# The order of loads around the first batch's attention products, and seven products in place of four tiles for the last group

## The chip, the cores and the metric

The kernel runs on one core of one Trainium2 chip. The metric is the device time of one execution in microseconds (us). The kernel before was timed in three runs: 520.41, 521.44 and 521.71 us, median 521.44 us. A separate execution was profiled.

## The reference

Four batches of 1024 tokens with 512 channels pass through one block, all in float32:

```python
mod = (silu(c) @ wmod).reshape(4, 6, 1, 512)          # sa, ca, ga, sb, cb, gb
h = layernorm(x) * (1 + ca) + sa
qf, kf = h @ Wq.T, h @ Wk.T                            # rank 64, the same for all heads
attn = softmax(qf @ kf.T)
x = x + ga * ((attn @ (h @ Wv.T)) @ Wo.T)
h = layernorm(x) * (1 + cb) + sb
x = x + gb * (sum_r(h @ factors[r]) / sqrt(8) + bias)   # eight factors of 512 x 512
```

`ga` and `gb` are first kept away from zero (at least 0.25 in size). All heads have the same scores, so attention is one matrix of 1024 x 1024 for each batch.

## The kernel before, in words

The kernel folds Wv and Wo into one matrix (`wvo`), and the eight factors into one sum (`fsum`). For a batch it makes LN1 (layer norm and modulation), the q and k projections, eight tiles of scores (128 tokens x 1024), softmax, P = the turned probabilities, Y = h(wvo*ga), O = P Y, then LN2 and F = h(fsum*gb). A tile is 128 tokens; tiles 0 to 3 of a batch are group 0, tiles 4 to 7 group 1.

**Products by sevens.** O and F are made in blocks of two by two with seven block products in place of eight (Strassen's scheme). For O a pair p = 0..3 of tiles has products (p,1), (p,5), (p,4), (p,6), (p,2), (p,3), (p,7); for F each group g has two pairs m = 0, 1. The seven share three PSUM banks: 1, 6, 7 and 4 accumulate one after another in bank "y" (which has two buffers, so the next pair's can begin), 5 and 3 in "q", and 2 in "x". After each product VectorE adds the bank's state to a quarter of x (L581 for O, L632 for F), so the next product of the same bank has to wait for that add. Products 5, 6 and 3 take sums of left blocks (`sum_probs` L502, `sum_h` L601: n = 0 for product 5, n = 1 for 6, n = 3 for 3; n = 2 overwrites the block that product 7 reads). Only the last batch's group 1 is made in another way: `f_tile` (L639) multiplies each of its four tiles plainly, four matmuls of 128x512 each, with one add of 128x512 (L648) and one store.

**Moves.** Transposing P or a normalised h takes a 32x32 transpose on VectorE (L491 for P, L378 for h) and then sixteen DMAs of 64 KB that move the 32x32 blocks (`move_blocks`, L374). They are issued by SyncE (SP), one queue, in program order. A batch has four moves of P (64 DMAs) and four of h (64 DMAs; the last two, of the last batch, are split between SP and ScalarE's queue). P and h moves of LN2 are made of 128 B packets.

**Buffers that tie things together.** The tag "pr" has three buffers: the probabilities of the four pairs and the staging tiles `st` of LN1 and LN2 rotate through them. So `st` of the next batch's group 0 takes the buffer of pair 1's probabilities, and group 1's that of pair 2, and ScalarE's first write there (L318, a sum over x) waits until that move of P has landed. Factors 2 and 3 live in two of the four "hT" buffers; LN2 of batch 0 takes these two buffers next.

**Order.** Every operation is put on a list with a beat (`at`, `pe`, `behind`), and `plan.run` sorts by beat; that order is the program order, hence the order of every engine's own queue. Engines run their queues in order. `behind` puts a tiny VectorE memset ("tick", L277) and a GpSimd copy of it ("mark", L279) ahead of GpSimd work, so that GpSimd doesn't start it before VectorE got there.

The loads that matter here, all in batch 0: SP issues x of batch 1 (eight DMAs of 256 KB, L114) at the end of `plan_start`, ahead of the P moves (L695). GpSimd (POOL) issues the factors (1 MB each, L261) and adds them to `fsum` (L264): factors 1 to 4 in `plan_start`, 5 to 7 in `plan_o` (L792 to L797). Factor 5 is loaded into factor 2's buffer, 6 into 3's, 7 into 2's again. `scale_w` (L286) makes the next batch's wvo*ga on POOL from `bc_ga`, a row that SP spreads over the partitions behind the P moves (L243). The reciprocal standard deviation of a layer norm (a power, L327 for LN1 and L339 for LN2) is taken on POOL, in its queue; for LN2 VectorE first adds epsilon (`rstd`, L337) and afterwards makes -mean*rstd (`center`, L344).

Of the kernel before, what the change touches and what calls it, by code (L numbers as in the profile page):

```python
# [37 lines left out]
def kernel(  # L38
# [52 lines left out]
    def psum_mm(name, tag=None):  # L91
        turn[0] += 1
        return psum(tag or "yqyx"[turn[0] % 4], 512, name)
# [160 lines left out]
    def load_factor(r):  # L254
        if r == 0:
            fac[r] = fsum
        elif r < 4:
            fac[r] = wide(*((wfp, "wf") if r == 1 else (hp, "hT")), f"factor_{r}")
        else:
            fac[r] = fac[{4: 1, 5: 2, 6: 3, 7: 2}[r]]  # L260
        nc.gpsimd.dma_start(out=fac[r], in_=factors[r].rearrange("(kc p) e -> p kc e", p=P))  # L261

    def add_factor(r, k):
# [67 lines left out]

    def stage(ln, b, g):
        st[ln, b, g] = prp.tile([P, NQ, KC, GT, Q], F32, tag="pr", name=f"st{ln}_{b}_{g}")

    def rstd(ln, b, g):
        v = small.tile([P, GT], F32, tag="rs_v", name=f"v{ln}_{b}_{g}")
# [299 lines left out]
            [a[:, k, ts(m, P)] for k in range(KH)], [f[:, k, :] for k in range(KH)], add,  # L636
        )

    def f_tile(b, t):  # L639

        g, j = divmod(t, GT)
        ps = psum_mm(f"ps_f_{b}_{t}")
        for kc in range(KC):
            nc.tensor.matmul(  # L644
                ps, hT[2, b, g][:, ds((kc * GT + j) * P, P)], fb[b][:, kc, :],
                start=(kc == 0), stop=(kc == KC - 1),
            )
        nc.vector.tensor_tensor(xt[b, t], ps, xt[b, t], ALU.add)  # L648

    def f_pair(g, m):  # L650
        return g * GT + m, g * GT + GT // 2 + m

    def store(b, t, queue):
        queue.dma_start(out=out[b, ts(t, P), :], in_=xt[b, t])  # L654

    def add_bias(b, t):
        nc.gpsimd.tensor_tensor(xt[b, t], xt[b, t], bcs["gbias", b], ALU.add)  # L657
# [3 lines left out]
    def plan_softmax(b, p, k):  # L661

        at(plan.now + 0.5, exponents, b, p, k)
        if k:
            at(plan.now + 7, turn_probs, b, p)
            at(plan.now + 8, move_probs, b, p)

    def plan_start():
        for g in range(2):
            s = 8.0 if g == 0 else 44.0  # L670
            for j in range(GT):
                at(s + 2 * j, stats, 1, 0, g * GT + j)
            at(s + 9, rstd, 1, 0, g)
            for j in range(GT):
                at(s + 10 + j, normalize_first, g * GT + j)
        pe(8, warm_up)
        for cc in range(KC - 1):
            pe(8, wvo_chunk, cc)
        pe(8, mod_products, [0, 1], "q")
        at(plan.now, mod_row, 1, nc.vector)  # L680
        at(plan.now, mod_row, 0, nc.scalar)
        pe(4, wvo_chunk, KC - 1, range(2))
        at(plan.now, wvo_out, 0)
        at(plan.now, wvo_out, 1)
        for m, plus in ((1, 1.0), (0, 0.0)):
            pe(1, channel_products, m)
            at(plan.now, channel, m, plus)
        pe(4, wvo_chunk, KC - 1, range(2, KC))
        for kc in range(KC):
            pe(1, turn_first, 0, kc)  # L690
            at(plan.now, first_out, 0, kc)
        at(plan.now, wvo_out, 2)
        at(plan.now, wvo_out, 3)
        for t in range(NT):
            at(plan.now + (22 if t < GT else 40), load_x, 1, t)  # L695
        for r in range(2):
            at(plan.now + 1, load_factor, r)
        at(plan.now + 21, after_gates)
        for r in range(1, 5):
            if r in (2, 3):  # L700
                at(plan.now + 21, load_factor, r)
            for h in range(2):
                at(plan.now + 14 * r + 8 + 6 * h, add_factor, r, ts(h, KC // 2))
            if r == 1:
                at(plan.now + 14 * r + 15, load_factor, 4)
        pe(8, project, 0, 0)
        at(plan.now, qk_out, 0, 0)
        for kc in range(KC):
            pe(1, turn_first, 1, kc)
            at(plan.now, first_out, 1, kc)  # L710
        pe(8, mod_products, [2, 3, 4, 5], "y")
        for m in (2, 5):
            at(plan.now, mod_row, m, nc.scalar)
            at(plan.now, gate_sign, m)
            if m == 2:
                at(plan.now, gate, m)
        for m in (3, 4):
            at(plan.now, mod_row, m, nc.scalar)
        at(plan.now + 0.1, gate_b)
        at(plan.now, publish, row(2), "ga")  # L720
        pe(8, project, 0, 1)
        at(plan.now, qk_out, 0, 1)
        pe(2, spread_first)
        for kc in range(KC):
            at(plan.now, scale_w, 0, kc, nc.vector)
# [39 lines left out]
    def plan_ln2(b, g, ready):  # L765

        for j in (GT - 2, GT - 1):
            at(ready, stats, 2, b, g * GT + j)
        at(ready + 0.5, rstd, 2, b, g)
        at(ready + 4, center, 2, b, g)  # L770
        for j in range(GT):
            eng = nc.scalar if b + 1 == B and (g or j % 2) else nc.vector
            at(ready + 5 + 2 * j, normalize, 2, b, g, j, eng)
        for c in range(NQ):
            at(ready + 13 + (2.6 if b + 1 == B else 2) * c, turn_h, 2, b, g, c)
        at(ready + (21.5 if b + 1 == B else 19.5), move_h, 2, b, g)
        for j in range(GT):
            behind(ready + (22 if b + 1 < B else 26) + 5 * j, add_bias, b, g * GT + j)
        for kc in range(KC):
            late = 46 + 4 * (kc // 2) * g if b + 1 < B else 31  # L780
            at(ready + late, shift_h, 2, b, g, kc, nc.scalar)

    def plan_o(b):
        s = plan.now
        if b + 1 < B:
            plan_ln1(b + 1, 0, s + 2, s + 20)
            plan_ln1(b + 1, 1, s + 21, s + 39)
            at(s, spread, "ga", b + 1)
            for kc in range(KC):
                behind(s + (92 if b == 0 else 60) + 6 * kc, scale_w, b + 1, kc, nc.gpsimd)  # L790
        if b == 0:
            at(s - 28, load_factor, 5)  # L792
            at(s + 14, load_factor, 6)
            at(s + 34, load_factor, 7)
            for r, beat in ((5, s + 3), (7, s + 48), (6, s + 74)):
                for kc in range(KC):
                    behind(beat + 6 * kc, add_factor, r, ts(kc, 1))  # L797
        at(s + 24, spread, "gbias", b)
        for n in range(4):
            at(s - (26 if b else 16) + 3 * n, sum_probs, b, 0, n)  # L800
            at(s + 2 + 4 * n if b else s + 2 * n, sum_probs, b, 1, n)
        for p in range(NP):
            if 0 < p < NP - 1:
                for n in range(4):
                    at(plan.now + 3 + 4 * n, sum_probs, b, p + 1, n)
            for n in (1, 5, 4, 6, 2, 3, 7) if p < NP - 1 else (1, 5, 4, 6, 2, 7, 3):
                if n != 4:
                    pe(4, o_product, b, p, n)
                elif p:
                    pe(4, o_product, b, p - 1, 4)  # L810
                    if p % 2:
                        for j in range(2):
                            at(plan.now + 2 + 4 * j, stats, 2, b, 2 * (p - 1) + j)
                    else:
                        plan_ln2(b, p // 2 - 1, plan.now + 2)
        pe(4, o_product, b, NP - 1, 4)
        plan_ln2(b, 1, plan.now + 1)

    def plan_f(b, groups):
        pairs = [(g, m) for g in groups for m in range(GT // 2)]  # L820
        queue = nc.gpsimd if b + 1 < B else nc.sync

        def done(t):
            at(plan.now + 2, store, b, t, queue)
            if b + 2 < B:
                at(plan.now + 12, load_x, b + 2, t, nc.gpsimd)

        def fourth(g, m):
            pe(2, f_product, b, g, m, 4)
            done(f_pair(g, m)[1])  # L830

        for i, (g, m) in enumerate(pairs):
            end = i + 1 == len(pairs)
            for n in (1, 5, 4, 6, 2, 3, 7) if not end else (1, 5, 4, 6, 2, 7, 3):
                if n != 4:
                    pe(2, f_product, b, g, m, n)
                    if n == 3:
                        done(f_pair(g, m)[0])
                elif i:
                    fourth(*pairs[i - 1])  # L840
        fourth(*pairs[-1])

    def plan_scale_f(b, spread_beat, beat, queue):
        at(spread_beat, spread, "gb", b, queue)
# [13 lines left out]
    for b in range(B):  # L858
# [15 lines left out]
        else:  # L874
            plan_scale_f(b, s - 170, s - 104, nc.gpsimd)
            plan_sums_f(b, s - 70, 6)
            plan_sums_h(b - 1, 1, s - 40, 5)
            plan_sums_h(b, 0, plan.now + 4, 3, nc.gpsimd)
            plan_f(b - 1, range(1, 2))
            plan_f(b, range(1))  # L880
            for t in range(GT, NT):
                pe(8, f_tile, b, t)
                at(plan.now + 2, store, b, t, nc.sync)
    with tc.manual_schedule():
        plan.run()

# [32 lines left out]
```

## Time and profile before

| what | us |
|---|---|
| runs of the kernel before, median of three | 521.44 |
| the profiled execution's own time | 521.12 |
| its span in the trace | 519.3 |
| PE (TensorE matmuls) busy | 503.8 |
| DVE (VectorE) busy | 366.9 |
| POOL (GpSimd) busy | 178.9 |
| ACT (ScalarE) busy | 172.1 |
| share of PE in the chain that ended last | 77% |
| share of SP's issues in that chain | 9% |

The trace starts when the first instruction starts. The page names engines PE, PEld (weight loads), DVE, ACT, POOL and SP; "SPq" is SP's queue issuing a DMA. "A<-B" in brackets after a row says how long the engine was idle before it and what ended the wait. PE is busy nearly throughout, so what matters is where it isn't, and at what clock it runs.

### The profile page before, as it was taken

What the parts mean: (1) busy time and instruction counts of PE and PEld (TensorE: products, weight loads), DVE (VectorE), ACT (ScalarE), POOL (GpSimd) and SP (SyncE); (2) the same over time, 40 slices, a digit from 0 to 9 for tenths busy, and PEclk for the clock granted to TensorE, in tenths of its full rate; (3) what the DMA queues carried; (4) which work ended last, traced back from release to release, by engine and by line L of the source; (5) the groups of instructions that cost most, each with busy time, mean ns of one, the idle gap of its engine ahead of it and who ended that gap; (6) DMA issues with size and microseconds to landing.
All of it is one profiled execution on the core that took longest, in us unless ns stands there. A gap on an engine that the chain in (4) does not pass through costs nothing.

```text
span 519.3 us, 6306 instructions
## 1 busy us (share of the span) xinstructions
PE 503.8 (97%) x1906; PEld 336.3 (65%) x1906; DVE 366.9 (71%) x728; ACT 172.1 (33%) x309; POOL 178.9 (34%) x240
## 2 busy tenths in 40 slices
PE   8999999779999999999999999999999999999997
PEld 4343437668733388888733388888733488888772
DVE  5358486289779966489679966589678975786631
ACT  1144434442265403452356304442256300012220
POOL 1027803335946013215535023215536015015620
PEclk9999999979999999999999999999999999999999
DMA  8977966964536679523536679533536776014542
GB/s 319 380 293 260 221 139 96 218 131 107 88 61 98 96 131 241 166 72 91 100 58 98 96 146 235 143 76 92 97 56 108 101 134 130 0 19 63 109 137 81
DMA packets 223154, 68.64 MB, mean 132 GB/s; under 512 B 206400, under 2 KB 206912, under 8 KB 223120
## 3 DMA queue, kind: packets, MB, share of 16 engines
q1 hardware_dynamic: 208112, 46.99, 46.1%
q0 software_dynamic: 5456, 19.14, 11.2%
q10 hardware_dynamic: 9552, 2.11, 2.1%
q8 instruction: 15, 0.25, 0.2%
q14 instruction: 19, 0.16, 0.1%
HBM read 28.33 MB, written 8.41 MB: 71 GB/s over the span
## 4 chain that ended last, share of the span: by engine, by line
PE 77%; SPq 9%; DVE 4%; ACT 3%; DMA 3%; issue 2%; POOL 0%; DVEq 0%; ACTq 0%; POOLq 0%
PE ps_o_y L564 20%; PE ps_y L521 14%; PE ps_o_q L564 9%; SPq L374 9%; PE ps_f_y L564 8%; PE ps_o_x L564 5%; PE ps_f_q L564 4%; PE ps_sc L468 4%; PE ps_qk L441 3%; PE ps_wvo L170 3%; PE ps_f L644 3%; PE ps_f_x L564 2%; PE ps_mod L189 1%; DMA hT<-st 1%; ACT st L356 1%
## 5 line engine op out<-in xcount | busy, mean ns | idle before, releaser
L521 PE MATMUL ps_y<-w,hT 128*128 128x512 f32 x256 | 117.0, 602 | 0.0
L521 PEld LDWEIGHTS ps_y<-w,hT 128*128 128x128 f32 x256 | 46.6, 190 | 66.7 <-issue 65.7
L394 ACT ACTIVATE hT<-hT,chan,chan 128x512 f32<-128x512 f32 x56 | 41.3, 803 | 99.3 <-DMA hT<-st 73.2
L564 PE MATMUL ps_o_y<-y,pt 128*128 128x256 f32 x256 | 61.2, 391 | 6.2 <-DVE x L581 6.2
L564 PEld LDWEIGHTS ps_o_y<-y,pt 128*128 128x128 f32 x256 | 50.4, 197 | 14.4 <-DVE x L581 6.6
L279 POOL COPY mark<-tick 1x1 f32<-1x1 f32 x72 | 17.2, 239 | 114.5 <-DVE tick L277 112.8
L482 ACT ACTIVATE pr<-ps_sc,nm 128x1024 f32<-128x1024 f32 x32 | 35.6, 1113 | 50.8 <-DMA pt<-pr 17.2
L581 DVE SCALAR_TENSOR_TENSOR x<-ps_o_y,ri,x 128x256 f32<-128x256 f32 x64 | 30.7, 480 | 30.8 <-PE ps_o_y L564 29.0
L654 POOL DMA_DIRECT2D out_dram<-x x24 | 13.3, 556 | 89.2 <-DVE x L632 88.9
L481 DVE TENSOR_REDUCE nm<-ps_sc 128x1 f32<-128x1024 f32 x32 | 38.3, 1213 | 6.5 <-PE ps_sc L468 6.5
L378 DVE STREAM_TRANSPOSE st<-st 128x512 f32<-128x512 f32 x56 | 37.8, 692 | 7.1 <-ACT st L356 6.9
L657 POOL TENSOR_TENSOR x<-x,bc_gbias 128x512 f32<-128x512 f32 x32 | 40.3, 1259 | 0.0
L491 DVE STREAM_TRANSPOSE pr<-pr 128x2048 f32<-128x2048 f32 x16 | 36.8, 2302 | 1.2 <-DMA hT<-st 0.6
L468 PE MATMUL ps_sc<-qk 64*128 64x512 f32 x128 | 35.4, 633 | 1.0 <-ACT pr L482 0.7
L632 DVE TENSOR_TENSOR x<-ps_f_y,x 128x256 f32<-128x256 f32 x56 | 23.4, 421 | 15.4 <-PE ps_f_y L564 15.4
L264 POOL TENSOR_TENSOR fsum<-fsum,factor 128x512 f32<-128x512 f32 (+1 forms) x20 | 33.7, 1696 | 0.2
L318 ACT ACTIVATE st<-x 128x512 f32<-128x512 f32 x24 | 14.9, 620 | 52.2 <-DMA x<-in_x_dram 40.1
L564 PE MATMUL ps_o_y<-yt,s 128*128 128x256 f32 x128 | 30.3, 380 | 1.1 <-DVE x L581 1.1
L339 POOL TENSOR_TENSOR r<-v,mhalf 128x4 f32<-128x4 f32 x10 | 11.7, 1170 | 55.7 <-DVE v L337 55.7
L306 DVE BATCH_NORM_STATS2 bn<-x 128x6 f32<-128x512 f32 x40 | 27.2, 679 | 4.4 <-DMA x<-in_x_dram 4.2
L564 PE MATMUL ps_o_q<-yt,s 128*128 128x256 f32 x128 | 30.2, 379 | 0.0
L564 PE MATMUL ps_o_q<-y,s 128*128 128x256 f32 x128 | 30.2, 379 | 0.0
(114 smaller groups left out, 839.7 us busy)
## 6 DMA issues: line engine op xcount, KB each, us to landing
pt<-pr SPq DMA_DIRECT2D x256, 64.0 KB, 2.3
hT<-st SPq DMA_DIRECT2D x208, 64.0 KB, 2.2
factor<-in_factors_dram POOLq DMA_DIRECT2D x7, 1024.0 KB, 8.7
wm<-in_wmod_dram SPq DMA_DIRECT2D x6, 1024.0 KB, 10.7
out_dram<-x POOLq DMA_DIRECT2D x24, 256.0 KB, 4.0
x<-in_x_dram POOLq DMA_DIRECT2D x16, 256.0 KB, 4.6
x<-in_x_dram SPq DMA_DIRECT2D x12, 256.0 KB, 7.2
out_dram<-x SPq DMA_DIRECT2D x8, 256.0 KB, 2.0
```

The source lines that it names most:

```text
L264: nc.gpsimd.tensor_tensor(fsum[:, k, :], fsum[:, k, :], fac[r][:, k, :], ALU.add)
L374: queues[r % len(queues)].dma_start(out=dst[ts(c, Q), r], in_=src[ts(r, Q), c])
L378: nc.vector.transpose(s, s)
L394: eng.activation(v, v, AF.Identity, bias=shift, scale=scale)
L468: nc.tensor.matmul(ps_sc[b, i][:, ts(h, 512)], qT[h * R : (h + 1) * R, ts(i, P)], kT[h * R : (h + 1) * R, :], start=True, stop=True,)
L481: nc.vector.tensor_reduce(nm, ps_sc[b, i], AX.X, ALU.max, negate=True)
L482: nc.scalar.activation(probs[b, p][:, :, k].rearrange("p c j e -> p j c e"), ps_sc[b, i].rearrange("p (j c e) -> p j c e", j=NT, c=NQ), AF ...
L491: nc.vector.transpose(v, v)
L521: nc.tensor.matmul(ps, h_rows(1, b, t, kc), wb[b][:, kc, :], start=(kc == 0), stop=(kc == KC - 1))
L564: nc.tensor.matmul(ps, left, right, start=(first and j == 0), stop=(j == len(lefts) - 1), skip_group_check=not first,)
L581: nc.vector.scalar_tensor_tensor(xi, ps, rinv[b][:, t : t + 1], xi, ALU.mult, ALU.add)
L657: nc.gpsimd.tensor_tensor(xt[b, t], xt[b, t], bcs["gbias", b], ALU.add)
```

## The change

It does five things.

1. **x of batch 1** is issued by SP in two lots of four: behind pair 0's P moves and behind pair 1's, in place of ahead of all of them.
2. **Factors 5, 6 and 7** are loaded later: 5 and 6 one after the other on POOL behind the LN1 constants of batch 1's group 0, and 7 behind factor 6's four adds, since it now takes factor 3's buffer (which 6 uses) and not factor 2's. The four `scale_w` of batch 1 move forward, between the adds of factor 5. POOL's order was: adds of 5; LN1's two sets of constants; adds of 7; LN2 group 0's power; adds of 6 mixed with bias adds and `scale_w`; LN2 group 1's power. It becomes: LN1 group 0's constants, loads 5 and 6, an add of 5, LN1 group 1's constants, `scale_w` and adds of 5 in turn, two adds of 6, LN2 group 0's power, two adds of 6, load 7, adds of 7 and bias adds in turn, LN2 group 1's power.
3. **Sums of P for pair 1** of batch 0 (`sum_probs`) come some beats later, so that the adds of the first products stand ahead of them on VectorE.
4. **The last batch's group 1** is made by seven products for each of its two pairs (`f_tile` is gone); its sums of h go to VectorE behind group 0's last add, the first pair's order is 1, 2, 5, 6, 3, 7, and the last tile is stored in two halves. The stores of batch 2's group 1, which POOL issues, move behind POOL's last bias adds.
5. **The last group's norm constants** are all made on POOL (`rstd_last`: add epsilon, negate the mean, power, product); VectorE's L337 and L344 drop out there.

```diff
-            fac[r] = fac[{4: 1, 5: 2, 6: 3, 7: 2}[r]]
+            fac[r] = fac[{4: 1, 5: 2, 6: 3, 7: 3}[r]]
...
+    def rstd_last(b, g):
+
+        v = small.tile([P, GT], F32, tag="rs_v", name=f"v2_{b}_{g}")
+        mean, var = (mv[2, b][:, ts(g, GT), i] for i in range(2))
+        nc.gpsimd.tensor_scalar(v, var, EPS, None, ALU.add)
+        n = small.tile([P, GT], F32, tag="rs_n", name=f"n2_{b}_{g}")
+        nc.gpsimd.tensor_scalar(n, mean, -1.0, None, ALU.mult)
+        r = rs[2, b, g] = small.tile([P, GT], F32, tag="rs_r", name=f"r2_{b}_{g}")
+        nc.gpsimd.tensor_tensor(r, v, mhalf, ALU.pow)
+        m = rm[2, b, g] = small.tile([P, GT], F32, tag="rs_m", name=f"m2_{b}_{g}")
+        nc.gpsimd.tensor_tensor(m, n, r, ALU.mult)
...
             at(plan.now + 8, move_probs, b, p)
+            if b == 0 and p < 2:
+                for t in range(GT):
+                    at(plan.now + 8.5, load_x, 1, p * GT + t)
...
-        for t in range(NT):
-            at(plan.now + (22 if t < GT else 40), load_x, 1, t)
...
-        at(ready + 0.5, rstd, 2, b, g)
-        at(ready + 4, center, 2, b, g)
+        if b + 1 == B and g:
+            at(ready + 0.5, rstd_last, b, g)
+        else:
+            at(ready + 0.5, rstd, 2, b, g)
+            at(ready + 4, center, 2, b, g)
...
-                behind(s + (92 if b == 0 else 60) + 6 * kc, scale_w, b + 1, kc, nc.gpsimd)
+                behind(s + (39 if b == 0 else 60) + 6 * kc, scale_w, b + 1, kc, nc.gpsimd)
         if b == 0:
-            at(s - 28, load_factor, 5)
-            at(s + 14, load_factor, 6)
-            at(s + 34, load_factor, 7)
-            for r, beat in ((5, s + 3), (7, s + 48), (6, s + 74)):
+            for r, load, add in ((5, 22, 36), (6, 34, 60), (7, 80, 90)):
+                at(s + load, load_factor, r)
                 for kc in range(KC):
-                    behind(beat + 6 * kc, add_factor, r, ts(kc, 1))
+                    behind(s + add + 6 * kc, add_factor, r, ts(kc, 1))
...
-            at(s + 2 + 4 * n if b else s + 2 * n, sum_probs, b, 1, n)
+            at(s + (2 if b else 5) + 4 * n, sum_probs, b, 1, n)
...
+            late = 32 if b + 2 == B and t >= GT else 1 if cols else 2
+            at(plan.now + late, store, b, t, queue, *cols)
...
+            order = (1, 5, 4, 6, 2, 7, 3) if end else (1, 5, 4, 6, 2, 3, 7)
+            if i == 0 and (b, g) == final:
+                order = (1, 2, 5, 4, 6, 3, 7)
...
+                    if n == 7 and end and (b, g) == final:
+                        done(f_pair(g, m)[1], ts(1, H))
...
-            plan_sums_h(b, 0, plan.now + 4, 3, nc.gpsimd)
+            plan_sums_h(b, 0, plan.now + 6, 3, nc.gpsimd)
+            plan_sums_h(b, 1, plan.now + 55, 1)
             plan_f(b - 1, range(1, 2))
             plan_f(b, range(1))
-            for t in range(GT, NT):
-                pe(8, f_tile, b, t)
-                at(plan.now + 2, store, b, t, nc.sync)
+            plan_f(b, range(1, 2))
```

More of the change, by code (lines that the diff above doesn't have):

```diff
@@ L637, in f_product, with store @@
         )
[L639 to L648, printed above, removed]
     def f_pair(g, m):
         return g * GT + m, g * GT + GT // 2 + m
-    def store(b, t, queue):
-        queue.dma_start(out=out[b, ts(t, P), :], in_=xt[b, t])
+    def store(b, t, queue, cols=slice(None)):
+        queue.dma_start(out=out[b, ts(t, P), cols], in_=xt[b, t][:, cols])
     def add_bias(b, t):
@@ L821, in plan_f, with done, fourth @@
         queue = nc.gpsimd if b + 1 < B else nc.sync
-        def done(t):
-            at(plan.now + 2, store, b, t, queue)
+        def done(t, *cols):
+            late = 32 if b + 2 == B and t >= GT else 1 if cols else 2
+            at(plan.now + late, store, b, t, queue, *cols)
             if b + 2 < B:
                 at(plan.now + 12, load_x, b + 2, t, nc.gpsimd)
-        def fourth(g, m):
+        def fourth(g, m, *cols):
             pe(2, f_product, b, g, m, 4)
-            done(f_pair(g, m)[1])
+            done(f_pair(g, m)[1], *cols)
+        final = (B - 1, 1)
         for i, (g, m) in enumerate(pairs):
             end = i + 1 == len(pairs)
-            for n in (1, 5, 4, 6, 2, 3, 7) if not end else (1, 5, 4, 6, 2, 7, 3):
+            order = (1, 5, 4, 6, 2, 7, 3) if end else (1, 5, 4, 6, 2, 3, 7)
+            if i == 0 and (b, g) == final:
+                order = (1, 2, 5, 4, 6, 3, 7)
+            for n in order:
                 if n != 4:
@@ L838, in plan_f @@
                         done(f_pair(g, m)[0])
+                    if n == 7 and end and (b, g) == final:
+                        done(f_pair(g, m)[1], ts(1, H))
                 elif i:
                     fourth(*pairs[i - 1])
-        fourth(*pairs[-1])
+        fourth(*pairs[-1], *([ts(0, H)] if (b, g) == final else []))
     def plan_scale_f(b, spread_beat, beat, queue):
```

## The prediction

> **What bounds the kernel now.** I read the page's busy row first (PE 503.8 of 519.3 us), then PE's waits, then the timeline around the longest.
>
> ```profile
> PE ps_o_y L564 <- DVE x L581: 7.3, 2, 6.2
> ...
> 97.78 0.63 ACT L318 ACTIVATE st<-x 128x512 f32<-128x512 f32 x1 [9.11 <-DMA pt<-pr]
> 105.12 1.30 DVE L378 STREAM_TRANSPOSE st<-st 128x512 f32<-128x512 f32 x2 [5.21 <-ACT st L356]
> 107.45 6.30 PE L564 MATMUL ps_o_y<-y,pt 128*128 128x256 f32 x16 [6.25 <-DVE x L581]
> ```
>
> PE has one real hole, in batch 0's attention: 1.1 us before 83.7 and 6.25 before 107.45. Read upward: PE waits for an add on DVE, which stands behind transposes, which wait for ACT, which idled 9.11 us until pair 2's P moves had landed and freed a "pr" buffer. The hole has a second price, in the clock. The table by windows (PE busy first, then the other engines, and at the end the granted clock, DMA share, GB/s) shows it:
>
> ```profile
> 101.00:105.50 4.50, 0.20 (x1) 0.00 (x0) 0.38 (x1) 4.47 (x10) 0.00 (x0) 1.00 0.61 85
> 107.50:112.50 5.00, 5.00 (x12) 4.02 (x13) 4.93 (x12) 2.93 (x4) 1.73 (x4) 0.50 0.76 179
> ```
>
> After the idle stretch PE runs five microseconds at half clock: sixteen matmuls take 6.30 us where they take 3.62 later, so 2.7 more. The hole is worth 1.1 + 6.25 + 2.7 = 10.0 us, and no more.
>
> Next, SP's queue, and how long P moves take to land, first undisturbed (72 to 88 us), then beside factor loads (91 to 102 us; columns: count, KB each, us to landing):
>
> ```profile
> 49.83 58.24 SPq L374 DMA_DIRECT2D pt<-pr  x64
> 108.11 0.62 SPq L243 DMA_DIRECT2D bc_ga<-rows_ga  x1
> 109.32 31.94 SPq L374 DMA_DIRECT2D hT<-st  x48
> ...
> pt<-pr SPq DMA_DIRECT2D x24, 64.0 KB, 2.3
> ...
> pt<-pr SPq DMA_DIRECT2D x8, 64.0 KB, 6.6
> ```
>
> SP issues without rest from 49.83 to 141.3. An undisturbed move is 0.67 us (0.63 and a 0.04 gap), so 64 would end at 92.9; they end at 108.1. In the chain of waits the 15 us of stall lie in three places: 4.5 up to 57.8 (x of batch 1 and factors 2 to 4 in flight), 4.6 about factor 5's load, 5.6 about factors 6 and 7, 0.4 elsewhere.
>
> **x and factors moved (parts 1 and 2).** I rebuild the end of the P moves. From 92.9 add eight x issues, which now stand between moves: 8 x 0.43 = 3.4. Add what the moves lose behind each lot of x: between nothing and 2.3 (half of 4.5); I take 0.5, twice, since moves use only 0.65 of the DMA share and catch up. Factor 4 alone in front of pair 0: 1.3 to 3.5, I take 2.4. Factors 5 and 6, back to back: 4.6 (the smallest share of one, 2.3, twice) to 9.2 (factor 5's, twice); I take the row of the other pair, 5.6. Sum 105.3; both ends give 102 to 113. So SP gains some 3 us of the 15, not 10.
>
> Does the hole close? Pair 2's moves are issued by 49.83 + 48 x 0.67 + 3.4 + 1.0 + 2.4 = 88.8. ACT's four LN1 sums start when Y is out (79.8), 1.46 each, to 85.7; POOL's constants take 1.8 more (106.64 to 108.45 now), so loads 5 and 6 leave at 87.5 and 88.3, and their data comes some 2 us later. Pair 2 thus lands at about 90 if just ahead of them, or near 96, as now. From landing to PE's restart is 9.7 us (97.78 to 107.45), and product (1,7) wants to start at 100.1: landing by 90.4 closes the hole; 96 leaves most of it and gains 1 to 2.
>
> Then what is late next. These rows are batch 0's LN2 powers on POOL, DVE waiting for them, ACT's shift of h, and the scores:
>
> ```profile
> 122.10 1.39 POOL L339 TENSOR_TENSOR r<-v,mhalf 128x4 f32<-128x4 f32 x1 [0.35 <-DVE v L337]
> 123.52 0.16 DVE L344 SCALAR_TENSOR_TENSOR m<-mv,r 128x4 f32<-128x4 f32 x1 [0.52 <-POOL r L339]
> ...
> 143.16 2.93 ACT L394 ACTIVATE hT<-hT,chan,chan 128x512 f32<-128x512 f32 x4 [8.92 <-DMA hT<-st]
> 144.23 1.02 POOL L339 TENSOR_TENSOR r<-v,mhalf 128x4 f32<-128x4 f32 x1 [0.17 <-DVE v L337]
> 145.28 0.16 DVE L344 SCALAR_TENSOR_TENSOR m<-mv,r 128x4 f32<-128x4 f32 x1 [1.20 <-POOL r L339]
> ...
> 148.15 2.51 PE L468 MATMUL ps_sc<-qk 64*128 64x512 f32 x8
> ```
>
> - *Group 0's power.* The first `scale_w` now waits on POOL for `bc_ga`, which SP issues behind all P moves and which takes 3.9 us to land: 105.3 + 3.9 = 109.2. Queued behind it, ahead of the power, are nine pieces (four `scale_w`, five adds) of 1.35 with their marks: 121.4, the power 1.1: 122.5, where it ends at 123.5 now. DVE holds the add of (2,3) behind it, and (3,5) needs that bank. It starts at 125.67 now and could at 124.6; so at 123.6, a gain of 2.1. If the first hole is closed, PE is there at 115.7 and idles 7.9 us: longer than the 6.25 that brought half clock, so 2.7 come back and the gain is -0.6.
> - *Group 1's power.* Two adds more, load 7 leaves at 125.2, lands 7.3 later (6.8 to 10.5 over all factors) at 132.5, then four adds and three bias adds, 9.5, and the power, 1.05: 143.0, against 145.25 now. The q and k copies of batch 1 stand behind it on DVE: gain 2.2.
> - *SP.* 105.3 + 1.2 (two spreads) + 31.9 + 2 (load 7 beside the last sixteen; 0 to 4.6) + 1.9 to land = 142.3, against 143.16: gain 0.9. ACT's copies of q and k stand behind that shift.
>
> The least holds, whether PE waited early or late: 0.9, or -0.6 with the clock. I take 0.5, bounds -4 (SP ends at 108 or later, and load 7 takes 10.5) to +10.
>
> [...]
>
> **Sums of P for pair 1 (part 3)** are hidden behind pair 0's products; the 1.1 before 83.67 is in the hole's price. If the cover goes, (1,5) waits at most 0.7, one sum.
>
> **The last group (parts 4 and 5).**
>
> ```profile
> 480.13 1.23 DVE L344 SCALAR_TENSOR_TENSOR m<-mv,r 128x4 f32<-128x4 f32 x1 [0.47 <-POOL r L339]
> 481.40 2.93 ACT L356 ACTIVATE st<-x,m,r 128x512 f32<-128x512 f32 x4 [3.67 <-DVE m L344]
> ...
> 498.16 2.93 ACT L394 ACTIVATE hT<-hT,chan,chan 128x512 f32<-128x512 f32 x4 [13.84 <-DMA out_dram<-x]
> ...
> 501.59 13.90 PE L644 MATMUL ps_f<-f,hT 128*128 128x512 f32 x32
> ...
> 515.59 0.69 DVE L648 TENSOR_TENSOR x<-ps_f,x 128x512 f32<-128x512 f32 x1 [2.74 <-PE ps_f L644]
> 516.31 0.33 SPq L654 DMA_DIRECT2D out_dram<-x  x1
> ```
>
> *Constants.* DVE's product took 1.23 us (0.16 elsewhere) beside a POOL sum. On POOL: two small operations of 0.2 to 0.4, the power 1.02, one of 0.2, with gaps 2.1 after the statistics at 478.9: 481.0, against 481.4. DVE is free of 1.4 us. PE's weight loads waited there for adds four times, 0.47, 0.24, 1.29 and 0.26; I take 0.7 of those 2.3 away (0 to 1.5). h is then ready before 501; POOL's stores of batch 2, now out of the move's way, take it to about 497, which gains nothing, as PE comes at 500.9.
>
> *Products.* Fourteen of 0.863 (row by row between 489 and 501) are 12.1, against 13.9. DVE is the rub: behind group 0's last add it has, before the add of (5), two sums, an add, two sums, an add; with 0.6 a sum and 0.37 an add and the start 0.6 after PE's, the add of 5 ends at 4.2, product 3 needs that bank and could start at 3.45: a wait of 0.85 (0 to 1.5). The later adds fit (0.42 in 0.86). So 12.95; then an add of 0.42 in place of 0.69, and a half store, which I give the 2.0 us of the whole. Gain 13.9 - 12.95 + 0.2 = 1.1. Together 1.8 (0.3 to 2.9).
>
> **Sum.** 521.12 - 0.5 - 1.8 = 518.8 for the profiled execution; the median of the runs lies 0.3 above it: **519.1 us**, its own range 517.5 to 520.5.
>
> **Rivals.**
>
> - *The hole closes and nothing takes its place.* P moves end by 100, so both powers and SP run 5 us earlier than in my sum, PE's waits stay under 4 us and the clock holds. For: the fewest stalls. Against: factors 5 and 6 leave beside pair 3's moves. Gain 6 to 10 and the tail 1.8: about 512. Chance 0.20.
> - *POOL becomes the bound, slower.* Load 7 can only leave when factor 6's adds are done, and group 1's power stands behind its landing. With the P moves ending at 108 and a landing of 10.5 the power ends 3 + 3 later than in my sum, at 149, 3.7 late; the idle PE pays 2.7 of clock a second time. Less the tail, 4 to 5 us slower: about 525. It decides from a power ending later than 147.1 (145.25 + 1.8). Chance 0.16.
> - *The change doesn't do what it says:* the hole only moves, and DVE eats the tail (three waits of 0.85 in place of one, which leaves 0.1): 520.5 to 521.5. Chance 0.24.
> - My forecast: 0.40.
>
> Measurement tells 0.3%, 1.6 us, from no change. Faster by more: 0.20, 0.32 of my own case, 0.04 of the third, 0.56. Within: 0.29. Slower: 0.15. The range leaves out half of the first rival and most of the second: 512 to 522.5.
>
> **What would show it.** Pair 2 landing near 90 or 96; P moves ending at 105; POOL idle until `bc_ga` lands near 109; PE's longest wait at (1,7) or (3,5) and 0.50 clock after it; group 1's power near 143; in the tail one PE wait under a microsecond, and 12.9 us of products. I am wrong if the P moves end near 100 or POOL's power passes 147.

## The result, and the profile after

Four runs of the changed kernel took 525.55 to 527.06 us, median 526.79; four of the kernel before, on the same chip, 521.58. The ratio is 1.0099 (95% interval 1.0076 to 1.0122): about 1% slower, where 0.5% faster was forecast. The profiled execution took 526.97 us, its span is 525.2 (before: 519.3).

Where the 5.9 us lie is found by setting the same PE rows of both timelines side by side, each counted from its first O product (78.98 before, 79.18 after). The q and k projection of batch 1 starts 58.78 later before, 65.56 after: **6.8 lost inside batch 0's attention**. The first F product starts at 103.86 and 111.52: 7.7 lost, 0.9 of it at the scores. From the last O product to the end of the span it is 45.33 before (473.97 to 519.3) and 43.38 after (481.82 to 525.2): **1.95 gained in the tail**. With 0.2 of a later start: 0.2 + 7.7 - 1.95 = 5.9.

PE's waits between 76 and 160 us (total, times, longest), where before had 7.3 in two:

```profile
PE ps_o_y L576 <- DVE x L593: 5.9, 1, 5.9
PE ps_o_q L576 <- DVE x L593: 3.3, 1, 3.3
PE ps_o_y L576 <- DVE tick L277: 2.6, 1, 2.6
```

The timeline of the same stretch:

```profile
100.49 0.63 ACT L318 ACTIVATE st<-x 128x512 f32<-128x512 f32 x1 [14.53 <-DMA pt<-pr]
100.54 0.69 DVE L522 TENSOR_TENSOR s<-pt 128x512 f32<-128x512 f32 x1 [8.59 <-DMA pt<-pr]
101.68 2.57 PE L576 MATMUL ps_o_q<-y,s 128*128 128x256 f32 x8 [3.34 <-DVE x L593]
...
107.83 1.31 DVE L390 STREAM_TRANSPOSE st<-st 128x512 f32<-128x512 f32 x2 [5.21 <-ACT st L368]
108.38 0.62 SPq L243 DMA_DIRECT2D bc_ga<-rows_ga  x1
110.17 5.20 PE L576 MATMUL ps_o_y<-y,pt 128*128 128x256 f32 x16 [5.92 <-DVE x L593]
117.01 1.26 POOL L264 TENSOR_TENSOR fsum<-fsum,factor 128x512 f32<-128x512 f32 x1
117.50 4.03 DVE L522 TENSOR_TENSOR s<-pt 128x512 f32<-128x512 f32 x1
118.22 0.17 POOL L279 COPY mark<-tick 1x1 f32<-1x1 f32 x1
118.36 1.26 POOL L289 TENSOR_TENSOR w<-wvo,bc_ga 128x512 f32<-128x512 f32 x1
119.71 1.26 POOL L264 TENSOR_TENSOR fsum<-fsum,factor 128x512 f32<-128x512 f32 x1
127.16 5.24 PE L576 MATMUL ps_o_y<-y,pt 128*128 128x256 f32 x16 [2.60 <-DVE tick L277]
```

Two things are seen. The old hole is still there, later and in two pieces: pair 2's P moves land at 100.5 (97.78 before), the first sum of pair 2 holds up DVE and so product (1,3) by 3.34, and (1,7) restarts 9.7 us after the landing, as before. And there is a **second hole** at (2,7): a sum of P that takes 0.69 elsewhere takes 4.03 at 117.50, and it ends 0.56 after the last of POOL's operations beside it (119.71 + 1.26). (The row at 127.16 names the tick; the add that product (2,7) needs stands just ahead of the tick on DVE and ends at 127.1.) Both holes are followed by reduced clock. The windows are the hole before (1,7), then the five microseconds behind it and behind the second (PE busy and the other engines; clock, DMA share and GB/s at the end):

```profile
104.30:110.10 5.80, 0.00 (x0) 0.00 (x0) 2.27 (x6) 4.89 (x11) 0.32 (x2) 0.50 0.65 104
110.20:115.20 5.00, 5.00 (x16) 4.21 (x17) 4.48 (x15) 2.29 (x4) 4.75 (x8) 0.70 0.68 177
127.20:132.20 5.00, 5.00 (x16) 4.19 (x17) 4.38 (x12) 0.70 (x1) 3.80 (x5) 0.69 0.34 82
```

The rows that I had named as "late next" all came 7 to 8 us later than before (there the powers end at 123.5 and 145.3, and the shift starts at 143.2):

```profile
129.04 1.39 POOL L351 TENSOR_TENSOR r<-v,mhalf 128x4 f32<-128x4 f32 x1
...
147.63 4.46 DVE L349 TENSOR_SCALAR v<-mv 128x4 f32<-128x4 f32 x1
150.76 2.93 ACT L406 ACTIVATE hT<-hT,chan,chan 128x512 f32<-128x512 f32 x4 [16.33 <-POOL x L658]
152.24 1.03 POOL L351 TENSOR_TENSOR r<-v,mhalf 128x4 f32<-128x4 f32 x1 [0.18 <-DVE v L349]
155.33 3.19 PE L480 MATMUL ps_sc<-qk 64*128 64x512 f32 x8
```

The tail: the one wait of the new products, and the last add.

```profile
513.14 1.13 PE L576 MATMUL ps_f_q<-f,sf 128*128 128x256 f32 x4 [0.66 <-DVE x L644]
...
522.08 0.42 DVE L644 TENSOR_TENSOR x<-ps_f_y,x 128x256 f32<-128x256 f32 x1 [0.44 <-PE ps_f_y L576]
```

### The profile page after: what moved, and what is told of

Same layout as the page of the kernel before. It is cut to its first block, busy times and chain, and to the rows that moved or that the text cites. A ratio compares the mean times of both kernels' runs of the same rounds, so it can differ in the third digit from the quotient of the medians.

```text
span 525.2 us, 6383 instructions
## 1 busy us (share of the span) xinstructions
PE 505.0 (96%) x1930; PEld 341.3 (65%) x1930; DVE 374.9 (71%) x740; ACT 172.3 (33%) x309; POOL 178.2 (34%) x243
## 4 chain that ended last, share of the span: by engine, by line
PE 74%; SPq 8%; DVE 7%; DMA 3%; issue 3%; ACT 3%; POOL 1%; DVEq 0%; ACTq 0%; POOLq 0%
PE ps_o_y L576 18%; PE ps_y L533 14%; PE ps_f_y L576 10%; PE ps_o_q L576 9%; SPq L386 8%; PE ps_f_q L576 5%; PE ps_o_x L576 4%; PE ps_sc L480 4%; PE ps_qk L453 3%; PE ps_wvo L170 3%; PE ps_f_x L576 2%; DMA pt<-pr 1%; PE ps_mod L189 1%; DMA hT<-st 1%; DVE st L390 1%
## 5 line engine op out<-in xcount | busy, mean ns | idle before, releaser
L644 DVE TENSOR_TENSOR x<-ps_f_y,x 128x256 f32<-128x256 f32 x64 | 26.9, 421 | 18.9 <-PE ps_f_y L576 18.9
L576 PE MATMUL ps_o_x<-y,pt 128*128 128x256 f32 x128 | 30.2, 379 | 0.0
L576 PE MATMUL ps_o_y<-yt,pt 128*128 128x256 f32 x128 | 30.2, 379 | 0.0
```

The lines of the kernel that those rows point to most:

```text
L576: nc.tensor.matmul(ps, left, right, start=(first and j == 0), stop=(j == len(lefts) - 1), skip_group_check=not first,)
```

## The experiments

The theories. **A**: loads 5 and 6 leave at 87.6 and 88.4, just ahead of pair 2's last moves, and catch them. **B**: POOL's order (constants and powers queued behind adds that wait for a tick) sets the end. **C**: DVE's sums of P are held while POOL works through a bunch of adds and `scale_w`. And part 1 itself, x in SP's chain.

In the table times count from each run's own first O product (it starts between 78.6 and 80.6); "pair 2" is the start of ACT's first sum behind its landing; the ratio is to the kernel before on the same chip. Single times of the kernel before spread from 518.4 to 524.7 on these chips, so differences under 1.5 us are read from the stages, and there too a stretch of half clock varies by about 1 us (58.8 and 57.7 with the same front: the sixteen matmuls behind the hole took 6.30 and 5.14).

| run | pair 2 | projection | first F | ratio of times (95%) |
|---|---|---|---|---|
| before | 18.8 | 58.8 | 103.9 | 1 |
| after | 21.3 | 65.6 | 111.5 | 1.0099 (1.0076 to 1.0122) |
| e1_tail_only | 18.9 | 57.7 | 105.5 | 0.9960 (0.9934 to 0.9987) |
| e2_x_back | 17.7 | 62.9 | 108.8 | 1.0024 (0.9993 to 1.0055) |
| e3_factors_back | 22.6 | 61.5 | 106.4 | 1.0015 (0.9985 to 1.0044) |
| e4_no_loads_5_6 | 12.7 | 59.5 | 105.3 | 0.9975 (0.9952 to 0.9998) |
| e5_scale_w_later | 21.4 | 62.9 | 108.8 | 1.0025 (0.9999 to 1.0052) |
| e6_loads_behind_pair2 | 12.9 | 63.4 | 109.4 | 1.0049 (1.0025 to 1.0073) |
| e7_all_three | 10.8 | 52.0 | 105.0 | 0.9986 (0.9962 to 1.0009) |
| e9_shift_later | 10.8 | 52.0 | 99.5 | 0.9873 (0.9819 to 0.9926) |
| e11_one_tick | 19.7 | 66.1 | 109.7 | 1.0024 (0.9993 to 1.0054) |
| e12_e9_one_tick | 10.0 | 50.1 | 96.8 | 0.9819 (0.9769 to 0.9868) |

**1. The parts one by one.** The diff is to the kernel after; e1 undoes parts 1, 2 and 3 together.

```diff
 e2: part 1 undone
-            if b == 0 and p < 2:
-                for t in range(GT):
-                    at(plan.now + 8.5, load_x, 1, p * GT + t)
+        for t in range(NT):
+            at(plan.now + (22 if t < GT else 40), load_x, 1, t)
 e3: part 2 undone
-            for r, load, add in ((5, 22, 36), (6, 34, 60), (7, 80, 90)):
-                at(s + load, load_factor, r)
+            at(s - 28, load_factor, 5)
+            at(s + 14, load_factor, 6)
+            at(s + 34, load_factor, 7)
+            for r, beat in ((5, s + 3), (7, s + 48), (6, s + 74)):
...
```

> Only the last group's seven products and its norm constants are changed against the kernel before (parts 4 and 5). In the trace after, the tail from the last O product to the end of the span is 1.95 us shorter than before. If that belongs to the tail alone, this kernel takes 521.6 - 1.95 = 519.6 us. If the tail only looks shorter because the late first half gave POOL and DVE other phases, it takes 520.5 or more.

> The kernel after with x of batch 1 back in front of all P moves (part 1 undone). Theory A (factor loads 5 and 6 catch the last moves of pair 2): the moves of pair 2 are issued some 3 us earlier and land before the factors' data, ACT's wait for pair 2 ends near 90 in place of 100.5, the hole before (1,7) goes and the time falls by 5 to 9, to 518 to 522. Theory C (DVE is held while POOL works through its bunched adds): the second hole near 127 stays and the time falls by 2 at most, to 525. If part 1 is the culprit by itself: 519.6, and pair 2 is still caught.

> The kernel after with factors 5 to 7 and scale_w loaded and added as before (part 2 undone); x stays behind the moves. Theories A, B and C all lay the loss on part 2: 519 to 520 us, 7 under the kernel after. If moving x into SP's chain is the culprit: 524 or more.

e1: 520.01 against 521.42, so the tail's gain is real (expected -1.95; measured -1.4 by the medians and -2.1 by the ratio, interval -3.4 to -0.7); its first F is late by a wait of 1.96 us at the scores, of which part 5 tells. e2 and e3 each stand between: x alone costs the projection 3.3 us (61.5 against the mean 58.2 of before and e1), the factor part alone 4.6, both 7.3. No theory that lays all on part 2 holds (for e3 I expected 519 to 520 us; it took 522.6): x in the chain delays pair 2 by 3.8 us by itself, with the loads in their old places. And with x back, pair 2 is *still* caught (17.7, not 10.8 as where the loads come behind it, e7 below) and the second hole stays as it was, which speaks for C. (For e2 I expected 518 to 522 us by A, 525 by C and 519.6 if x alone did it; 523.5 is none of these, though nearest to C. For e3, 522.6 also lies under the 524 that I had set for x as the culprit.) Part 3, the later sums of P for pair 1, stays in both runs, and no run takes it away alone; but in neither e2, e3 nor the kernel after does PE wait between 76 us and its first wait for pair 2 (101.7 in the kernel after).

The rows of e2:

```profile
106.02 5.91 PE L576 MATMUL ps_o_y<-y,pt 128*128 128x256 f32 x16 [6.50 <-DVE x L593]
...
123.68 5.41 PE L576 MATMUL ps_o_y<-y,pt 128*128 128x256 f32 x16 [2.61 <-DVE tick L277]
```

**2. The loads taken away.** e4 leaves out the transfers of factors 5 and 6; their adds stay and take factors 2 and 3 once more.

```diff
-                at(s + load, load_factor, r)
+                at(s + load, load_factor if r == 7 else same_factor, r)
```

> The kernel after without the transfers of factors 5 and 6 (the adds stay and take factors 2 and 3 once more, so part of the sum is wrong). Theory A: pair 2 lands near 92.5, pair 3 is not stalled and ends near 100, the waits 3.3 and 5.9 and their half clock (2.3) go, 11 us less: 515 to 516. Theory B (POOL's order: constants and powers queued behind adds that wait for DVE's tick) and theory C (DVE held beside POOL's adds): POOL's queue is the same, so the later hole and the late power stay, and at most the 3 us of the first hole are gained: 523 to 525.

```profile
91.61 0.63 ACT L321 ACTIVATE st<-x 128x512 f32<-128x512 f32 x1 [5.90 <-DMA pt<-pr]
...
101.29 3.72 PE L579 MATMUL ps_o_y<-y,pt 128*128 128x256 f32 x16 [1.48 <-DVE x L596]
...
111.61 5.64 DVE L525 TENSOR_TENSOR s<-s,pt 128x512 f32<-128x512 f32 x1
...
119.81 6.71 PE L579 MATMUL ps_o_y<-y,pt 128*128 128x256 f32 x16 [5.39 <-DVE tick L280]
```

A is right about its own hole: pair 2 lands 8.6 us earlier, and 1.48 us of wait is left. But the run took 521.1, not 515 to 516 (nor the 523 to 525 of B and C): a sum of P is now held for 5.64 us, and the second hole has grown to 5.39 us with 6.71 in place of 3.62 behind it. Two causes in a row, and the second takes back what the first gives.

**3. The second hole: order or bunch?**

```diff
 e5: batch 1's scale_w behind load 7
-                behind(s + (39 if b == 0 else 60) + 6 * kc, scale_w, b + 1, kc, nc.gpsimd)
+                behind(s + (81 + 2 * kc if b == 0 else 60 + 6 * kc), scale_w, b + 1, kc, nc.gpsimd)
 e6: loads 5 and 6 behind pair 2, first adds behind LN1's constants
-            for r, load, add in ((5, 22, 36), (6, 34, 60), (7, 80, 90)):
-                at(s + load, load_factor, r)
+            behind(s + 28, load_factor, 5)
+            at(s + 28.2, load_factor, 6)
+            at(s + 80, load_factor, 7)
+            for r, add in ((5, 40), (6, 61), (7, 90)):
...
-                behind(s + (39 if b == 0 else 60) + 6 * kc, scale_w, b + 1, kc, nc.gpsimd)
+                behind(s + (43 if b == 0 else 60) + 6 * kc, scale_w, b + 1, kc, nc.gpsimd)
```

> The kernel after with one edit: batch 1's four scale_w stand behind load 7 and no longer between the adds of factor 5, so that POOL's adds come one tick apart. The stage from the first O product to the projection of q and k takes 65.6 us in the kernel after, 58.8 before. Theory C (DVE's sums of P are held while POOL works without a gap): the sum that took 4.03 us takes under 1.9, the second hole (2.6 us at product (2,7)) and its half clock (1.6) go, the stage takes 61 us and the run 522 to 523. Theory B (the order of POOL's constants and powers sets it): LN1's constants still stand behind the first add, the hole stays and the run takes 526 or more.

> The kernel after with loads 5 and 6 behind a tick that follows DVE's first sum for pair 2, hence behind the landing of pair 2, and LN1's constants of group 1 ahead of factor 5's first add; scale_w and adds stay in turn. Theory A: pair 2 lands near 92 in place of 100.5 and the waits of 3.3 and 5.9 us go (stage 11 us shorter: 54.5). Theory C besides: the bunch of adds and scale_w still holds DVE, a hole near (2,7) of 3 to 6 us with half clock stays as in the run without the loads: stage 59 to 60, run 520 to 521. If pair 3, now the one caught, becomes the late one, the hole is at the sums of pair 3 and the same size.

PE's waits of e5 with the sum of P that took 4.03 in the kernel after, and two rows of e6:

```profile
PE ps_o_y L576 <- DVE x L593: 6.1, 2, 5.4
PE ps_o_q L576 <- DVE x L593: 3.5, 1, 3.5
```

```profile
117.59 0.69 DVE L522 TENSOR_TENSOR s<-pt 128x512 f32<-128x512 f32 x1
```

```profile
115.70 7.09 DVE L522 TENSOR_TENSOR pt<-pt 128x512 f32<-128x512 f32 x1 [1.03 <-issue]
...
123.24 2.08 PE L576 MATMUL ps_o_y<-y,pt 128*128 128x256 f32 x4 [8.55 <-DVE x L593]
```

In e5 the second hole is gone, though LN1's constants still stand behind the first add; in e6, where they stand ahead of it, a sum is held for 7.09 us and PE waits 8.55. So C, and not B, for the second hole. e5 took 522.8 us, as C had it. (Its projection is at 62.9 and not 61: the half clock behind its first hole lasted longer, 6.61 for the sixteen matmuls against 5.20; granted clock 0.66 from 100 to 120 us, 0.74 in the kernel after.) e6 took 523.9, not 520 to 521, and its stage 63.4, not 59 to 60: the hold was larger than in e4. Pair 3 landing late isn't the reason: its first sum started at 108.85, long before the hole. In e6 two waits of DVE (1.40 and 1.03, "issue" in the rows) end just behind a mark of POOL: a tick has four buffers, which the marks free, so POOL's queue may reach DVE that way too. The kernel after has a longer one at the end of O: DVE's add at 144.16 had waited 2.60 ("issue") and started when the mark at 143.95 was done, which stood on POOL behind an add that waited 3.59 for factor 7. This is read from the order of the rows, not tested.

**4. How long is DVE held?** Three kernels measure it alone, each in one profiled execution.

> Not the block but a measurement: six operations of a kind on DVE alone, then the same six while POOL runs four 128x512 sums without a gap, for sums of two SBUF tiles, normalising (one SBUF tile, two scalars), 32x32 transposes, statistics, adds from PSUM, and a 128x4 operation. Theory C: of the sums the first one beside POOL ends only when POOL's four are done (4 to 5.5 us), and the others take 0.69 as alone; adds from PSUM, transposes and statistics aren't held. Rival (the two engines share bandwidth): every operation beside POOL is longer by the same part, 20 to 100%, and none takes over 2 us.

> A measurement again: three sums (or 128x4 operations) on DVE beside four POOL sums, with and without the 1x1 copy (the mark) between POOL's sums, and with POOL's sums independent or in place. In the last such run, without marks, each sum on DVE was held for one POOL sum (1.58 to 1.74 us). If the marks keep DVE out, the first DVE operation beside marked sums takes 4 to 6 us and the others 0.7; without marks each takes 1.6 to 1.8. If in-place sums do it, the in-place series without marks shows the 4 to 6. If neither: 1.6 to 1.8 everywhere, and what holds DVE for 4 to 7 us in the kernel is something else.

> A measurement: three sums on DVE beside six POOL sums without a gap, in four orders (w: three products to separate tiles; f: in-place sums of three tiles; w and f in turn; f: six in-place sums of one tile), first without and then with a 1x1 mark ahead of each. In the kernel with one tick for four, w and f in turn without marks held one sum of P for 4.47 us; in the last measurement independent sums without marks held it for 1.6 to 1.7. If the alternation of two input pairs is what keeps DVE out, w-f without marks shows 4 us or more and w alone 1.7. If only marks and independence matter: without marks 1.4 to 1.9 in all four orders, and with marks 5 or more in the first three and 1.9 in the last. If neither pattern comes out, the rule stays open.

From e8: a sum of two SBUF tiles beside POOL sums (0.69 alone), a transpose and an add from PSUM beside them (0.66 and 0.40 alone), and six 128x4 operations alone and beside them:

```profile
11.70 1.74 DVE L60 TENSOR_TENSOR d<-a,b 128x512 f32<-128x512 f32 x1
32.46 0.66 DVE L64 STREAM_TRANSPOSE d<-a 128x512 f32<-128x512 f32 x1
48.71 0.40 DVE L62 TENSOR_TENSOR c<-ps,a 128x256 f32<-128x256 f32 x1
53.41 1.17 DVE L68 TENSOR_SCALAR v<-bn 128x4 f32<-128x4 f32 x6
55.34 4.81 DVE L68 TENSOR_SCALAR v<-bn 128x4 f32<-128x4 f32 x6
```

From e13: POOL's products and adds in turn without marks, then products with a mark ahead of each, then adds that depend on one another with marks:

```profile
33.16 1.47 DVE L60 TENSOR_TENSOR c<-a,b 128x512 f32<-128x512 f32 x1
...
54.09 9.48 DVE L60 TENSOR_TENSOR c<-a,b 128x512 f32<-128x512 f32 x1
55.05 0.17 POOL L108 COPY mark<-tick 1x1 f32<-1x1 f32 x1
55.18 1.25 POOL L111 TENSOR_TENSOR w<-a,b 128x512 f32<-128x512 f32 x1
...
89.97 1.56 DVE L60 TENSOR_TENSOR c<-a,b 128x512 f32<-128x512 f32 x1
```

These rows show a hold and not one stretch for all. In e8 the sums of two SBUF tiles took 1.58 to 1.74 beside POOL's (0.69 alone), each ending 0.54 to 0.56 behind the end of a POOL sum; normalising took 1.23 to 1.48 (0.53 alone), ending 0.28 or 0.29 behind one. Transposes took 0.66 to 0.68 (0.66 to 0.69 alone), adds from PSUM 0.40 (0.40 alone), and seven statistics 5.06 (six alone 4.32, 0.72 each in both). Without marks DVE got in after each POOL sum (1.47 to 1.75 us a sum, in all four orders of e13), and POOL's sums were longer too (1.70, against 1.25 for the first and for those behind DVE's last). So what I expected of e8 for theory C, a first sum of 4 to 5.5, didn't come, nor did a stretch of all operations alike, as the rival had it. With a 1x1 mark ahead of each of POOL's independent sums it didn't get in at all, and POOL's sums stayed at 1.25: one sum on DVE was held for 9.48 us, through six marked sums and the one behind them, and for 5.61 through four in e10, as I had expected there. Where the marked sums depended on each other, it was 1.56 to 1.88 again. That is the third outcome that I had set for e13: marks and independence, not two input pairs in turn.

**5. All three mended, and what was late next.** e7 is the kernel after with x back, e5's `scale_w`, e6's loads and adds, and pair 3's sums of P eight beats later. e9 adds one edit:

```diff
             late = 46 + 4 * (kc // 2) * g if b + 1 < B else 31
+            late += 24 if b == 0 and g == 0 else 0
```

> The kernel after with x of batch 1 ahead of the P moves again, loads 5 and 6 behind pair 2's landing, scale_w behind load 7, and the sums of P for pair 3 eight beats later. If A, C and x in SP's chain are the whole of it: pair 2 lands near 90, no hole over 2 us before the projection, full clock, stage 49 to 51 us, and with the tail a run of 509 to 512. If something else is late next (pair 3 caught by the loads, or batch 1's Y waiting for scale_w): 514 to 519, with one hole of 4 to 7 us at that place.

> The run with all three edits, and ACT's shift of batch 0's LN2 group 0 (an h that is not needed before F) 24 beats later, so that it no longer stands ahead of ACT's copies of q and k. There PE waited 4.4 us for q and k and then ran 4.4 us longer at half clock. Theory: ACT's copies stand behind that shift, which waits for the end of SP's chain of moves (139.6 us): without it scores start near 141.5 at full clock and the run takes 511 to 513. Rival: DVE's own copy of q is just as late, behind the held epsilon operation and LN2's power (139.8): scores start near 142.5 to 144 and the run takes 515 to 517.

e7's landing and its scores:

```profile
89.62 0.63 ACT L318 ACTIVATE st<-x 128x512 f32<-128x512 f32 x1 [4.01 <-DMA pt<-pr]
...
141.46 2.93 ACT L406 ACTIVATE hT<-hT,chan,chan 128x512 f32<-128x512 f32 x4 [8.28 <-DMA hT<-st]
144.41 0.58 ACT L469 COPY qk<-ps_qk 64x512 f32<-64x512 f32 x1
145.03 0.68 DVE L470 COPY qk<-ps_qk 64x512 f32<-64x512 f32 x1 [4.26 <-ACT qk L469]
145.76 4.99 PE L480 MATMUL ps_sc<-qk 64*128 64x512 f32 x8 [4.40 <-DVE qk L470]
```

Pair 2 lands at 89.6, no wait before the projection exceeds 1.13 us, and the projection starts 6.8 us earlier than before: the hole is closed. Yet the run took 520.1 against 520.9 (I had expected 509 to 512, or up to 519), no better than the tail alone. ACT's copies of q and k stand behind its shift of LN2's h, which waits for the last move that SP issues (end 139.6), and SP issued these moves without rest (106.86 to 139.6; 109.32 to 141.3 before), though PE was 6.8 us ahead. The 6.8 us came back as a wait of 4.40 and reduced clock (0.74 from 140 to 160 us). With the shift moved behind those copies (e9) the run takes 515.5 against 521.7. I had expected 511 to 513, or 515 to 517 if DVE's own copy was as late. The time is the rival's, but the trace doesn't show its mechanism: DVE's copy of q did start late (142.31), yet PE was busy until then and didn't wait for it. Scores start at 143.04, 62.6 behind the first O product (66.9 in e7, and 62.7 in the theory's 141.5), at full clock (1.00 is the mean granted clock of this profile); the first O product itself starts 1.6 later in this profile. What is left behind the scores' start is two waits of PE for ACT's exponentials, 1.1 and 1.0, where before has one of 0.7.

**6. Fewer marks.**

```diff
-                    behind(s + add + 6 * kc, add_factor, r, ts(kc, 1))
+                    (at if kc else behind)(s + add + 6 * kc, add_factor, r, ts(kc, 1))
```

The same edit is made to batch 1's `scale_w`.

> The kernel after with a tick and mark only ahead of the first of each four scale_w and adds; POOL's order and the bunch stay. If the marks between POOL's sums keep DVE out (4.03 us for one sum of P), each sum of P is held for 1.8 us at most, the second hole (2.6 us and its half clock) goes and the run takes 521.5 to 523.5. If POOL's bunch by itself does it, the hole stays: 526 to 527.5.

> The shift-later run with one tick and mark ahead of each four scale_w and adds. If marks keep DVE out: the 1.1 us waits before (3,4) and at the end of O and the 4.46 us of epsilon fall under 2 us, 1 to 3 us less than the shift-later run. If not: the same within 0.5 us.

e11 decides little: the median of 523.0 us is what I expected of the marks, but its ten times spread from 519.7 to 526.7, and the profiled execution, to which the row of the table belongs, is the slowest. In it a sum of P was still held for 4.47 us, beside three POOL operations without a mark between them, and PE waited 1.55 and 2.78. So marks lengthen the hold where it was measured alone, and aren't needed for it in the block; what else decides stays open. In e12, where the bunch is spread already, no sum of P takes over 0.70, the largest wait before the projection is 0.69, and the run takes **512.4 us against 521.7**: faster than both kernels. It is 3.1 less than e9, where I expected 1 to 3 from the marks, and PE's waits before the projection fall from 2.6 in all to 1.2. Whether the epsilon operation of group 1 fell under 2 us, as expected, isn't shown: POOL's power behind it began 6.85 us behind the projection's start (137.49 and 130.64), against 7.52 in e9 (139.95 and 132.43). So fewer marks help here, and by which way isn't shown.

## Why the prediction was wrong, step by step

*The hole and its price* were read rightly: it is one chain from pair 2's landing to (1,7), 9.7 us long in both kernels, and reduced clock follows it (0.50 before, 0.70 after, in five microseconds). The forecast failed in two of the steps that follow.

*"Pair 2 thus lands at about 90 ... or near 96"* **failed**: 100.5. The chain of waits shows the place, SP's issues and then the transfer:

```profile
89.20 0.81 SPq L386
90.05 2.67 SPq L386
92.83 7.61 DMA pt<-pr
100.49 0.73 ACT st L318 x2
```

I took the later case from a row with one load ahead of the moves; here two loads of 1 MB left together, and the moves were later besides. I saw that the loads could catch pair 2's last moves, but priced that no higher than the landing of the kernel before, so that the hole could only shrink or stay. The terms of SP's sum: the eight x issues took 4.3 us (3.4 taken), the moves lost 2.3 and 1.0 behind the lots of x (0.5 each), factor 4 cost 0.25 (2.4), factors 5 and 6 7.6 (5.6). They add up to 108.4 for the end of the P moves, which is within my 102 to 113 and 3 us over what I took. The end mattered less than I thought; the landing of pair 2 inside the chain was what PE waited for.

*"Group 0's power ... nine pieces of 1.35"* **failed**, and this was the larger part. Of the 6.8 us, (1,7) restarts 2.5 later than before and its half clock gives 1.1 back; the other 5.4 come behind it. (Taking the second hole away in e5 gained 2.7, with 1.4 more of half clock behind the first.) I counted the nine pieces as a queue on POOL alone, ending in a power at 122.5, and put their hold on DVE at nothing. The power ended at 130.4. Half of the 7.9 us is a late start: the first `scale_w` began at 112.95 and not 109.2, behind `bc_ga` (issued at 108.4) and LN1's constants. The other half is that the nine pieces took 16.0 us and not 12.2, as POOL waited 1.70, 0.71 and 1.10 for ticks of DVE. And DVE was late because the pieces held its sums of P, which stand ahead of the adds that PE waits for: PE's wait came at (2,7), ahead of the power, and (3,5), where I had put it, didn't wait. I had the evidence in the profile of before: two sums of P there took 1.51 and 1.78 us, each beside a POOL operation, and LN2's epsilon of 0.17 took 3.98:

```profile
118.01 1.78 DVE L510 TENSOR_TENSOR pt<-pt 128x512 f32<-128x512 f32 x1
...
140.11 3.98 DVE L337 TENSOR_SCALAR v<-mv 128x4 f32<-128x4 f32 x1
```

I read the 1.23 us product in the tail as a collision with POOL and didn't carry that to the attention stage. The bounds (-4 to +10) contained no such mechanism; the region lost 7.7.

*The least of three gains holds* was the right rule. e7 shows it: the hole closed, and SP's chain, which gained little (139.6 against 141.3), decided. So the first rival's gain of 6 to 10 us didn't come from closing the hole alone; it needed the shift moved as well (e9).

*The rival that POOL becomes the bound* was near in time (525) and right in sign, but not in mechanism: load 7 landed 6.6 us after it left, no later than I took, and PE was already over 6 us late when it left at 136.07. Group 1's power at 153.3 passed my threshold of 147.1 as a consequence; the wait of 2.60 for a mark and the epsilon of 4.46 stand ahead of it on DVE, and I had priced neither. e5 and e6 speak against the order as the cause.

*The tail* was right: 1.95 us against 1.8. From the first F product of the tail to the last group it is 25.31 against 25.89 (0.58; 0.7 taken); from there to the end of the last add 13.64 against 14.69 (1.05); the half store ends 0.3 sooner. The wait at product 3 was 0.66 (0.85).

*The half clock.* The kernel before gave me two points: clock 0.50 behind 6.25 us of wait, 1.00 behind 1.1. The runs add some between them. A wait of 2.60 us in the kernel after, with 0.3 us of wait shortly ahead of it, was followed by clock 0.69 and sixteen matmuls in 5.24 us in place of 3.62; behind e2's 2.61 they took 5.41, and behind e11's 2.78 eight took 3.39 in place of 1.89. Behind waits of 1.48 (e4), 1.55 (e11) and 1.64 (e6) sixteen took 3.72, and with e1's wait of 1.96 the clock was 1.00 from 140 to 160 us. What waits between 1.96 and 2.60 do, no run shows. That the clock holds with waits under 4 us, as the first rival had it, no run shows; the waits of 2.60 to 2.78 speak against it.

## What to carry to other kernels

Price GpSimd work not only by its own queue but by the VectorE operations that run beside it (here a sum of 0.69 us took 4.03): look in the profile for rows whose longest member is a multiple of the median, and see which engine ended just before them. When a hole of PE is to be closed, follow every other chain to the next common point (here the scores) first, since the smallest of the gains is what arrives. A load that is put off should be placed behind the landing of the small moves that something waits for, not by the clock of the plan (here two loads just ahead of them put the landing off by 8.6 us).

## What the runs showed of the hardware that I had not expected

- One 128x512 sum on VectorE, 0.69 us alone, took 9.48 us beside seven GpSimd operations, six of them independent with a 1x1 copy ahead of each, and 1.5 to 1.75 without the copies. In the block such copies weren't needed for a hold of 4.47. Even a 128x4 operation (0.17 elsewhere) was held: 4.46 us in the kernel after.
- Two loads of 1 MB that leave together just ahead of the last 64 KB moves put off the landing by 8.6 us (21.3 against 12.7 behind the first O product, with and without them), where the 24 moves issued from 72 to 88 us in the kernel before took 2.3 us (median).
- A wait of PE of 2.60 us was followed by clock 0.69 in the five microseconds behind it.
